# Beta written to the outputs ahead of time and added onto by transfers; two sums of x's parts moved from VectorE to ScalarE and adding transfers

## The chip, the cores and the metric

The kernel runs on one core of a Trainium2 chip, in float32. A time is the device time of one execution in microseconds (us). A figure given as a median is over several executions. The trace is of one further execution taken with the hardware profiler, and it has a time of its own. Engines are named as the profile names them: PE (TensorE), DVE (VectorE), ACT (ScalarE), POOL (GpSimd) and SP (SyncE). PEld is PE's loading of weights. A `q` after an engine's name (SPq, POOLq) means its instruction queue, for instructions such as a transfer's issue.

## The reference

Two layers of cross attention over a batch of eight. `x` is (8, 100, 1024): eight batches of 100 query rows. `ctx` is (8, 1444, 512): 1444 context rows per batch.

```python
# layer 0
Q = x @ Wq + bq;  K = ctx @ Wk + bk;  V = ctx @ Wv + bv
w = softmax(Q K^T / 32, over the context rows)
x = x + (w V) @ Wo + bo
# layer 1, with weights of its own
q, k, v = x @ Wq + bq, ctx @ Wk + bk, ctx @ Wv + bv
w = softmax(q k^T / 32, over the 100 query rows)
y = w v + x
out = (y - mean(y)) * rsqrt(var(y) + 1e-6) * gamma + beta      # over the 1024 features
```

`gamma` and `beta` are vectors of 1024 values, the same for every row.

## The kernel before

**Folded weights.** No K or V of 1444 rows is made. The kernel first multiplies weight matrices with each other: `qk0` = Wq Wk^T of layer 0, `vo0` = Wv Wo of layer 0, `qk1` = Wq Wk^T of layer 1 (`weight_products`, in this order; `qk1`'s multiplications come after layer 0's queries). The features of x then meet the 512 features of the context directly: `queries` computes g = W^T x + u for all 800 query rows, `scores` multiplies g with the context, `weighted_rows` multiplies the softmax weights with the context rows, and `project0` or `project1` carries the result back to 1024 features.

**x lies transposed.** `xT` holds x as 128 partitions by 8 chunks of features by 800 rows, so a block of it has features on the partitions. `project0` adds onto `xT` in place, and layer 1's `untransposed` brings each batch back to rows, as a tile `z` of 100 rows by 1024.

**Products with seven multiplications.** Most products are computed as two-by-two blocks with seven block products in place of eight (Strassen's scheme in Winograd's form), which costs sums of blocks beforehand. For `queries` the left blocks A are parts of the folded weights and the right blocks B are four parts of `xT`: B11 and B21 are the first 400 rows (two halves of the features), B12 and B22 the second 400 rows. The sums on the right are T1 = B12 - B11, T2 = B22 - T1, T3 = B22 - B12, and T4 = B21 - T2, which is written over T1. Each has 128 partitions by 1600 elements, 800 KB. T1 and T2 lie in two tiles of the tag `AT`, which the product `vo0` uses just before for sums of its own (`vo_s` in the trace). Layer 0's order in `queries` on PE is: product X from A11 and B11 (16 matmuls named `g_x`), a nested seven-product form of A12 times B21 (`g_z_...`), product Y from S1 and T1 (`g_y`), a further accumulation onto X from S2 and T2 (`g_x`), then the rest. The nested form makes small sums of its own on DVE (in the tile `g_t`, as T1 and T2 also show up in the trace, since both names begin with `g_t`; the shape tells them apart: 128x1600 against 128x400 and 128x256).

**Adding transfers.** The kernel has a helper, `transfer_added(to, t)` (line 572), that issues from POOL a DMA transfer which adds `t` onto `to` in SBUF. It sums scaled rows of weights with it: ACT scales (`scaled_sum`, line 578), the transfers add.

**What sets the order of the work.** PE runs its instructions in the order in which the program writes them (`manual_schedule`). For the other engines and for the transfer queues, a planner orders instructions by its own estimates of when each is ready. It may deviate from the written order: `wv1`'s load, written after those of gamma, beta and `bv1`, is issued ahead of them in the trace. `keep_in_program_order`, and `vector.in_order = True` for DVE, hold instructions so marked in their written order among themselves. Every engine runs its own instructions one after the other, so an instruction that waits holds up all that stands behind it on that engine.

**The end of layer 1.** For each batch, `untransposed` transposes `xT` on PE and DVE makes `z`. For batches 0 to 6 `normalise` (line 1201) then works on `z`: DVE takes mean and variance (`bn_stats`, `bn_aggr`), POOL raises the variance to -0.5 (`rstd`, line 1210), DVE subtracts the mean and multiplies with gamma (line 1211). Then, for batches 0 to 5, ACT multiplies with `rstd` (line 1216) and POOL adds beta (line 1217). For batch 6 DVE does both in one instruction (line 1214). The result is written to `out` by a transfer from POOL's queue (batches 0 to 3) or from SP's (batches 4 to 6). `finish` is called so that batches 0 to 2 are finished while batch 4 is worked on, batch 3 during batch 5, and batches 4, 5 and 6 while batch 7's weighted rows are multiplied. Batch 7 has a path of its own, `project_last` (line 1235). PE multiplies in three parts (`ol`: 384, 512 and 129 columns), DVE makes the mean and then `centred` part by part, ACT squares and sums each part (line 1264), POOL raises to -0.5 (`rstd_last`, line 1272), and DVE applies it with beta in two halves, each written by a transfer of its own (from SP and from ACT).

**Loading gamma and beta.** Both come into SBUF, spread over 128 partitions, with transfers from POOL's queue (line 1357), as does `bv1` (line 1359), when layer 1's queries begin. They lie in two tiles named `vectors_0` and `vectors_1`. `wv1`, 2 MB, is loaded in the same place of the program (line 1361).

Of the kernel before, what the change touches and what calls it, by code (L numbers as in the profile page):

```python
# [26 lines left out]
AF = mybir.ActivationFunctionType  # L27
ALU = mybir.AluOpType
# [4 lines left out]
B, T, E = 8, 100, 1024  # L33
# [15 lines left out]
SETS = (range(0, 4), range(4, 7), range(7, 8))  # L49
# [6 lines left out]
def two_layer_cross_attention(ctx: ExitStack, tc: tile.TileContext, a: dict, out: bass.AP):  # L56
    nc = tc.nc
# [16 lines left out]
    def unit(name):  # L74
        return stream.tile([P, E + L], F32, tag="unit", name=name)
# [104 lines left out]
    def combine(to, x, y, op, engine=vector):  # L180
        for t, p, q in zip(to, x, y):
            engine.tensor_tensor(t, p, q, op)
# [389 lines left out]
    def transfer_added(to, t):  # L572
        nc.gpsimd.dma_start(out=to, in_=t, accum_op=ALU.add)
# [85 lines left out]
    def queries(layer, w, u, between=None):  # L659

        H, nb, h = EC // 2, 2, GT // 2
        A11, A12, A21, A22 = ([w[:, k * H : (k + 1) * H, j * 256 : j * 256 + 256]] for j in range(2) for k in range(2))
        B11, B21, B12, B22 = ([xT[:, k * H : (k + 1) * H, g * GT : g * GT + GT]] for g in range(2) for k in range(2))
        S1, S2 = (
            [(unit if layer else row)(f"g{layer}_s{n}")[:, :E].rearrange("p (c l) -> p c l", c=H)] for n in (1, 2)
        )
        dst = [None, None]  # L670

        def put(r, g, banks):
            for j in range(2):
                c = 2 * r + j
                nc.scalar.activation(dst[g][:, c, :], banks[j][:, :GT], AF.Identity, bias=u[:, c : c + 1])  # L675

        def add(r, g, banks):
            for j in range(2):
                to = dst[g][:, 2 * r + j, :]
                vector.tensor_tensor(to, to, banks[j][:, :GT], ALU.add)  # L680

        def parts(R, G):
            def part(r, c, ps):
                return dst[G][:, 2 * R + r, c * h : c * h + h], ps[:, :h]

            def put(r, c, ps):
                c0 = 2 * R + r
                nc.scalar.activation(*part(r, c, ps), AF.Identity, bias=u[:, c0 : c0 + 1])

            def add(r, c, ps):  # L690
                to, got = part(r, c, ps)
                vector.tensor_tensor(to, to, got, ALU.add)

            return put, add

        def pair(n):

            return [(bank2 if layer and n == "y" else bank)(f"g{layer}_{n}{j}") for j in range(2)]

        def product(banks, lhs, rhs, fresh):  # L700
            half_product(banks, lhs, rhs, fresh, nb, GT)

        t = None

        def inner(n, lhs, rhs, put, add, right=None, at=0, left=None):
            spare = bank if layer else bank2
            return inner_product(f"g{layer}_{n}", lhs, rhs, nb, GT, t[:, at:], put, add, right, left, spare=spare)

        def four(t):

            return [[t[:, n, :].rearrange("p (i t) -> p i t", i=2)] for n in range(4)]

        def steps():
            nonlocal t
            S3, S4 = A21, A12
            if layer:
                combine(S1, A21, A22, ALU.add)
                yield
                combine(S2, S1, A11, ALU.subtract)
                yield  # L720
                combine(S3, A11, A21, ALU.subtract)
                yield
            T1, T2 = ([wide(f"g{layer}_t{n}")] for n in (1, 2))
            if layer:
                combine(T1, B12, B11, ALU.subtract)
                yield
            t = unit(f"g{layer}_t")
            T3 = [work.tile([P, LC, GT], F32, tag="gT", name=f"g{layer}_t3", bufs=3)]
            dst[:] = [work.tile([P, LC, GT], F32, tag="gT", name=f"g{layer}T_{g}", bufs=3) for g in range(2)]
            X = pair("x")  # L730
            product(X, A11, B11, True)
            put(0, 0, X)
            yield
            vector.in_order = True
            if layer == 0:

                rooms = t[:, :E].rearrange("p (n c l) -> p n c l", n=4, c=2)
                rooms = [[rooms[:, n]] for n in range(4)]
                _, more = parts(0, 0)
                Z = inner("z", A12, B21, more, more, four(T3[0]), left=rooms)  # L740
                combine(S1, A21, A22, ALU.add)
                combine(T1, B12, B11, ALU.subtract)
                run(Z)
                combine(S2, S1, A11, ALU.subtract)
                combine(T2, B22, T1, ALU.subtract)
                vector.in_order = False
                yield
                vector.in_order = True
                combine(S3, A11, A21, ALU.subtract)
                combine(T3, B22, B12, ALU.subtract)  # L750
            Y = pair("y")
            product(Y, S1, T1, True)
            put(1, 1, Y)
            if layer:

                vector.in_order = False
                yield
                vector.in_order = True
                S4 = A11
                combine(S4, A12, S2, ALU.subtract)  # L760
                _, more = parts(0, 0)
                Z = inner("z", A12, B21, more, more, four(T3[0]))
                combine(T2, B22, T1, ALU.subtract)
                run(Z)
                combine(T3, B22, B12, ALU.subtract)
            else:
                combine(S4, A12, S2, ALU.subtract)
            combine(T1, B21, T2, ALU.subtract)
            vector.in_order = False
            yield  # L770
            product(X, S2, T2, False)
            put(0, 1, X)
            yield
            vector.in_order = True
            V = half_steps(X, S3, T3, False, nb, GT)
            for n, _ in enumerate(inner("w", A22, T1, *parts(1, 0))):
                next(V)
                if layer:
                    yield
                if layer == 0 and n == 1:  # L780
                    between()
                elif layer == 0 and n == 3:

                    add(0, 1, Y)
                    _, more = parts(0, 1)
                    Q = inner("q", S4, B22, more, more, four(T2[0]), E)
            if layer == 0:
                next(Q)
                run(V)
                yield  # L790
                run(islice(Q, 4))
                add(1, 0, X)
                add(1, 1, X)
                run(Q)
                vector.in_order = False
            else:
                run(V)
                add(1, 0, X)
                add(1, 1, X)
                vector.in_order = False  # L800
                yield
                product(Y, S4, B22, False)
                add(0, 1, Y)
            yield

        return dst, steps()


# [392 lines left out]
    def normalise(s):  # L1201
        b, z = s["b"], s["z"]
        stats = small.tile([T, 2, 6], F32, tag="stats", name=f"stats_{b}")
        for j in range(2):
            nc.vector.bn_stats(stats[:, j, :], z[:, j * 512 : (j + 1) * 512])
        mv = small.tile([T, 2], F32, tag="mv", name=f"mv_{b}")
        nc.vector.bn_aggr(mv, stats.rearrange("p a n -> p (a n)"))
        rstd = small.tile([T, 1], F32, tag="rstd", name=f"rstd_{b}")
        nc.vector.tensor_scalar(rstd, mv[:, 1:2], EPS, None, ALU.add)
        nc.gpsimd.tensor_tensor(rstd, rstd, mhalf[:T], ALU.pow)  # L1210
        nc.vector.scalar_tensor_tensor(z, z, mv[:, 0:1], gamma[:T], ALU.subtract, ALU.mult)
        if b == B - 2:

            nc.vector.scalar_tensor_tensor(z, z, rstd, beta[:T], ALU.mult, ALU.add)
        else:
            nc.scalar.activation(z, z, AF.Copy, scale=rstd)  # L1216
            nc.gpsimd.tensor_tensor(z, z, beta[:T], ALU.add)  # L1217

        (nc.gpsimd if b < SETS[1][0] else nc.sync).dma_start(out=out[b], in_=z)

    def finish(s):

# [134 lines left out]
        nc.gpsimd.dma_start(out=t, in_=a[f"L1_xattn_{name}"].partition_broadcast(P))  # L1357
    for j, t in enumerate(bv1):
        nc.gpsimd.dma_start(out=t, in_=a["L1_xattn_bv"][j * 512 : (j + 1) * 512].partition_broadcast(P))
    wv1 = weights.tile([P, LC, E], F32, tag="w", name="wv1")  # L1360
    nc.gpsimd.dma_start(out=wv1, in_=a["L1_xattn_Wv"].rearrange("(c p) e -> p c e", p=P))  # L1361

# [54 lines left out]
```

## Time and profile before

| What | Value |
|---|---|
| Time, median of 3 runs | 633.31 us (632.94 to 633.76) |
| The profiled execution's own time | 633.67 us |
| Its span, first to last instruction | 631.6 us |
| Granted clock of PE | 0.996 of full |
| PE busy | 621.8 us (98%), 4142 matmuls |
| DVE busy | 482.4 us (76%) |
| ACT busy | 175.4 us (28%) |
| POOL busy | 101.5 us (16%) |
| Moved by DMA | 139.84 MB, 221 GB/s over the span |
| Beta added by POOL (line 1217) | 6 instructions, 2.36 us each |

The span is the profiled execution from its first to its last instruction, and the execution's own time is 2.1 us more. "Busy" counts only instructions at work. A wait is listed with the instruction that waited, on the left of an arrow, and the one that ended its wait, on the right. In a timeline a row gives start and duration in us, then engine, line, operation, output and inputs, shapes and how many instructions the row merges; a bracket gives the idle time before it and what ended it. A helper's line stands for all that go through it: line 96 is every DVE instruction issued through `vector`, line 163 every matmul of a block product. Tiles appear by name with their numbers left out.

### The profile page before, as it was taken

The numbers are of one execution on the slowest core, as the hardware profiler recorded it, in microseconds if no ns is written. First come the engines' busy times: TensorE is split into PE (matmuls) and PEld (weight loads), VectorE is DVE, ScalarE is ACT, GpSimd is POOL, SyncE is SP. The second block draws the span as 40 slices with busy tenths as digits, with TensorE's granted clock in tenths as the row PEclk, the third lists the DMA queues.
The fourth block names the chain that finished last, engine by engine and source line by source line (L and its number), as shares of the span: only waits on it lengthen the run. The fifth ranks groups of instructions, "written<-read, shape, count | busy, mean of one in ns | idle before, by whom it ended". The sixth has DMA issues, their size and how long they took to land.

```text
span 631.6 us, 10604 instructions
## 1 busy us (share of the span) xinstructions
PE 621.8 (98%) x4142; PEld 534.8 (85%) x4142; DVE 482.4 (76%) x993; ACT 175.4 (28%) x403; POOL 101.5 (16%) x135
## 2 busy tenths in 40 slices
PE   9999999999999999999999999999999999999994
PEld 8886467688986999999989666757999999999992
DVE  2977789996875797666758686968777659898886
ACT  1333112324304234423230001113433240328302
POOL 2110101112230000000000001008111220544052
PEclk9999999999999999999999999999999999999998
DMA  9969988336999799888942308266889990697202
GB/s 283 285 146 312 306 233 273 68 80 113 198 326 380 281 315 307 320 302 308 310 160 84 105 0 328 94 195 193 303 303 310 315 311 11 203 338 256 97 22 84
DMA packets 52952, 139.84 MB, mean 221 GB/s; under 512 B 4450, under 2 KB 8802, under 8 KB 52902
## 3 DMA queue, kind: packets, MB, share of 16 engines
q1 hardware_dynamic: 46792, 120.85, 55.7%
q0 software_dynamic: 5712, 17.84, 13.0%
q8 instruction: 33, 0.54, 0.3%
q10 hardware_dynamic: 398, 0.47, 0.2%
q14 instruction: 17, 0.14, 0.1%
HBM read 123.36 MB, written 3.28 MB: 201 GB/s over the span
## 4 chain that ended last, share of the span: by engine, by line
PE 96%; DVE 1%; issue 1%; POOL 1%; ACT 0%; DVEq 0%; POOLq 0%
PE s L929 25%; PE A L900 25%; PE qk_x L163 7%; PE o_x L163 5%; PE g_x L163 4%; PE vo_x L163 3%; PE o_y L163 3%; PE g_y L163 3%; PE qk_y L163 2%; PE qk_z L163 2%; PE o_z L163 1%; PE o_w L163 1%; PE qk_w L163 1%; PE vo_y L163 1%; PE vo_z L163 1%
## 5 line engine op out<-in xcount | busy, mean ns | idle before, releaser
L900 PE MATMUL A<-w,c 120*128 120x100 f32 (+1 forms) x1536 | 249.7, 265 | 0.0
L900 PEld LDWEIGHTS A<-w,c 120*128 120x128 f32 (+1 forms) x1536 | 218.0, 190 | 2.8
L96 DVE STREAM_TRANSPOSE w<-prob 32x384 f32<-32x384 f32 (+1 forms) x256 | 143.7, 561 | 27.9 <-ACT prob L968 9.7
L929 PE MATMUL s<-cT,g1T 128*100 128x131 f32 (+2 forms) x592 | 122.8, 296 | 0.0
L929 PE MATMUL s<-cT,g0T 128*100 128x131 f32 (+2 forms) x592 | 122.7, 296 | 0.0
L929 PEld LDWEIGHTS s<-cT,g1T 128*100 128x100 f32 x592 | 78.4, 167 | 8.6 <-issue 0.3
L929 PEld LDWEIGHTS s<-cT,g0T 128*100 128x100 f32 x592 | 78.2, 167 | 8.4 <-PE c L599 0.4
L941 ACT ACTIVATE prob<-s,c 100x393 f32<-100x393 f32 (+2 forms) x64 | 34.5, 560 | 110.5 <-PE s L929 97.3
L1117 ACT ACTIVATE w<-w,negmax 120x100 f32<-120x100 f32 (+1 forms) x96 | 34.8, 364 | 83.0 <-DVE negmax L96 83.0
L961 DVE TENSOR_REDUCE maxima<-prob 100x1 f32<-100x394 f32 (+3 forms) x32 | 16.5, 528 | 24.3 <-ACT prob L941 24.0
L1361 POOL DMA_DIRECT2D wv<-in_L_xattn_Wv x1 | 0.8, 772 | 192.5 <-PE o_x L163 192.5
L163 PE MATMUL qk_x<-qk 128*128 128x256 f32 x128 | 30.2, 384 | 0.0
L1136 POOL TENSOR_TENSOR part<-w 120x500 f32<-120x500 f32 x8 | 10.9, 1366 | 112.8 <-PE s L929 42.3
L163 PEld LDWEIGHTS qk_x<-qk 128*128 128x128 f32 x128 | 23.7, 194 | 3.1 <-ACT qk L437 0.2
L675 ACT ACTIVATE g1T<-g_x,k 128x400 f32<-128x400 f32 x4 | 2.4, 594 | 68.5 <-PE g_x L163 68.4
L1117 ACT ACTIVATION_READ_ACCUMULATOR w<-w,negmax 120x1 f32 (+1 forms) x96 | 17.9, 187 | 0.0
L96 DVE TENSOR_TENSOR xT<-xT,o_x 128x400 f32<-128x400 f32 (+1 forms) x32 | 15.8, 538 | 2.2 <-PE o_x L163 2.0
L1194 PE MATMUL z<-ident,xT 128*100 128x128 f32 x64 | 16.3, 273 | 0.0
L1217 POOL TENSOR_TENSOR z<-z,vectors 100x1024 f32<-100x1024 f32 x6 | 14.1, 2358 | 8.1 <-ACT z L1216 8.1
L1198 DVE SCALAR_TENSOR_TENSOR z<-vectors,r,z 100x512 f32<-100x512 f32 x16 | 11.8, 740 | 4.8 <-PE z L1194 4.8
L163 PE MATMUL vo_x<-vo 128*128 128x512 f32 x32 | 15.3, 595 | 0.0
L965 ACT ACTIVATE prob<-prob,negmax 100x1444 f32<-100x1444 f32 x8 | 12.0, 1499 | 11.2 <-DVE negmax L963 11.2
(431 smaller groups left out, 995.7 us busy)
## 6 DMA issues: line engine op xcount, KB each, us to landing
cT<-in_ctxT SPq DMA_DIRECT2D x64, 722.0 KB, 6.9
c<-in_ctx SPq DMA_DIRECT2D x48, 768.0 KB, 9.0
c<-in_ctx SPq DMA_DIRECT2D x16, 512.0 KB, 6.4
vo<-in_L_xattn_Wo SPq DMA_DIRECT2D x8, 512.0 KB, 9.6
qk<-in_L_xattn_WqT SPq DMA_DIRECT2D x8, 512.0 KB
qk<-in_L_xattn_WqT SPq DMA_DIRECT2D x15, 256.0 KB, 5.9
c<-in_ctx SPq DMA_DIRECT2D x16, 224.0 KB, 5.5
xT<-in_xT SPq DMA_DIRECT2D x2, 1600.0 KB
```

Source lines behind the costliest of these rows:

```text
L96: ins = getattr(nc.vector, op)(*args, **kw)
L163: nc.tensor.matmul(banks[n // per][:, n % per * width : (n % per + 1) * width], lhs[i][:, n * P : (n + 1) * P], rhs[i], start=(fresh and i ...
L900: nc.tensor.matmul(ps[:, k * T : (k + 1) * T], c[m // CQ][:r, m % CQ, k * P : (k + 1) * P], w[:r, m, :], start=(m == 0 and k == 0), stop=( ...
L929: nc.tensor.matmul(banks[n // per][:T, cuts[n] - o : cuts[n + 1] - o], q[:, k, t0 : t0 + T], cT[k][:, cuts[n] : cuts[n + 1]], start=(k == ...
L941: nc.scalar.activation(p[:, part], ps[:T, : part.stop - part.start], AF.Identity, bias=key_bias[layer][:T, b : b + 1], scale=SCALE,)
L961: nc.vector.tensor_reduce(maxima[:, n : n + 1], p[:, part], AX.X, ALU.max)
L965: nc.scalar.activation(p, p, AF.Exp, bias=negmax, accum_out=total)
L1117: nc.scalar.activation(w[:r, m0 + m, :], w[:r, m0 + m, :], AF.Exp, bias=negmax[:r, m : m + 1], accum_out=total[:r, m : m + 1])
L1136: add(part, w[:MR, 0:5, :], w[:MR, 5:10, :], ALU.add)
L1194: nc.tensor.transpose(ps[:T, e * P : (e + 1) * P], xT[:, 4 * j + e, b * T : (b + 1) * T], ident)
L1198: nc.vector.scalar_tensor_tensor(z[:, half], bv1[j][:T], s["r"], ps[:T, :], ALU.mult, ALU.add)
L1217: nc.gpsimd.tensor_tensor(z, z, beta[:T], ALU.add)
```

## The change

Two things are changed.

1. **Beta.** Right after the loads of gamma, beta and `bv1`, seven transfers from POOL's queue write the beta tile, 100 rows of 1024 equal rows, into `out` for batches 0 to 6. In `normalise` the addition of beta is gone for all seven: ACT multiplies with `rstd` (also for batch 6), and a transfer from POOL's queue adds `z` onto what stands in `out`. No output is written from SP's queue in `normalise` any more. Batch 7 stays as it was.
2. **Sums in layer 0's queries.** T1 = B12 - B11 and T2 = B22 - T1 are no longer made by DVE. ACT writes -B11 into T1, an adding transfer adds B12; ACT writes -T1 into T2, an adding transfer adds B22. The two ACT instructions are marked to keep their order, and they are written ahead of the first product of the queries. Layer 1's queries are unchanged.

```diff
@@ queries(): steps, after T1 and T2 are taken
+            if layer == 0:
+                tc.keep_in_program_order(nc.scalar.activation(T1[0], B11[0], AF.Copy, scale=-1.0))
+                transfer_added(T1[0], B12[0])
+                tc.keep_in_program_order(nc.scalar.activation(T2[0], T1[0], AF.Copy, scale=-1.0))
+                transfer_added(T2[0], B22[0])
@@ queries(): layer 0, the nested product
                 combine(S1, A21, A22, ALU.add)
-                combine(T1, B12, B11, ALU.subtract)
                 run(Z)
                 combine(S2, S1, A11, ALU.subtract)
-                combine(T2, B22, T1, ALU.subtract)
@@ normalise()
-        if b == B - 2:
-            nc.vector.scalar_tensor_tensor(z, z, rstd, beta[:T], ALU.mult, ALU.add)
-        else:
-            nc.scalar.activation(z, z, AF.Copy, scale=rstd)
-            nc.gpsimd.tensor_tensor(z, z, beta[:T], ALU.add)
-
-        (nc.gpsimd if b < SETS[1][0] else nc.sync).dma_start(out=out[b], in_=z)
+        nc.scalar.activation(z, z, AF.Copy, scale=rstd)
+
+        nc.gpsimd.dma_start(out=out[b], in_=z, accum_op=ALU.add)
@@ after the loads of gamma, beta and bv1
+    for b in range(B - 1):
+        nc.gpsimd.dma_start(out=out[b], in_=beta[:T])
```

## The prediction

> **What bounds the kernel now.** I read first the chain that ended last, then PE's waits, then timelines around the two places that the change touches. The chain, by engine:
>
> ```profile
> PE 96%; DVE 1%; issue 1%; POOL 1%; ACT 0%; DVEq 0%; POOLq 0%
> ```
>
> All of PE's listed waits (total, times, longest):
>
> ```profile
> PE warm L108 <- DVE ones L105: 1.1, 1, 1.1
> PE g_z_x L163 <- DVE g_t L96: 0.4, 1, 0.4
> ```
>
> PE is the bound until its last matmul ends at 623.3. Time can be won only from the 0.4 us wait and from the tail of 8.3 us behind that matmul, and lost wherever PE is made to wait.
>
> The wait lies in layer 0's queries; the 128x1600 row is T1, which the change takes off DVE:
>
> ```profile
> 104.72 1.81 DVE L96 TENSOR_TENSOR g_t<-xT 128x1600 f32<-128x1600 f32 x1
> ...
> 106.45 0.35 DVE L96 TENSOR_TENSOR g0T<-g0T,g_z_x 128x200 f32<-128x200 f32 x1
> 106.72 0.56 DVE L96 TENSOR_TENSOR g_t<-xT,g_t 128x400 f32<-128x400 f32 x1
> 107.21 0.42 DVE L96 TENSOR_TENSOR g_t<-g_t,qk 128x256 f32<-128x256 f32 x1
> ...
> 107.68 0.94 PE L163 MATMUL g_z_x<-g_t,g_t 128*128 128x200 f32 x4 [0.42 <-DVE g_t L96]
> ```
>
> The tail; the L1217 row is batch 5's beta, the L1211 row batch 6, `mean` and `centred` batch 7:
>
> ```profile
> 617.17 2.35 POOL L1217 TENSOR_TENSOR z<-z,vectors 100x1024 f32<-100x1024 f32 x1 [1.86 <-ACT z L1216]
> ...
> 617.46 3.15 DVE L1211 SCALAR_TENSOR_TENSOR z<-z,mv,vectors 100x1024 f32<-100x1024 f32 x1
> ...
> 618.81 4.48 PE L1259 MATMUL ol<-wv,A1T 128*100 128x512 f32 x16
> ...
> 619.49 1.53 POOL L1210 TENSOR_TENSOR rstd<-rstd,mhalf 100x1 f32<-100x1 f32 x1
> ...
> 620.53 0.20 DVE L96 SCALAR_TENSOR_TENSOR mean<-ol,last 100x1 f32<-100x1 f32 x1
> ...
> 621.05 1.28 DVE L1214 SCALAR_TENSOR_TENSOR z<-z,rstd,vectors 100x1024 f32<-100x1024 f32 x1 [0.31 <-POOL rstd L1210]
> ...
> 623.56 1.00 DVE L96 SCALAR_TENSOR_TENSOR centred<-ol,mean,z 100x512 f32<-100x512 f32 x2
> ```
>
> Two transfers in the list of issues, an adding one and beta's load (last number: us to landing):
>
> ```profile
> vo_L_xattn_bv<-prob POOLq DMA_DIRECT2D x1, 512.0 KB, 6.9
> ```
>
> ```profile
> vectors<-in_L_xattn_beta POOLq DMA_DIRECT2D x1, 512.0 KB, 12.8
> ```
>
> **What the Trainium skill says.** "SBUF — State Buffer", section "Who interferes with whom": a DVE instruction with two SBUF inputs contends with a POOL instruction that reads SBUF, and the loser blocks fully. The trace agrees: L1211 (z and gamma) takes 3.15 us beside the L1217 addition, 1.27 us at its shortest. "DMA: Bandwidth & Descriptors", section "SWDGE vs HWDGE vs iDMA": accumulating transfers go only from GpSimd, so all seven outputs join POOL's queue. The same page's "Rules for kernel authors" wants an accumulating transfer to wait for the earlier one on the same bytes; beta's writes precede the additions by over 140 us, so that wait should be spent; no run here shows it yet.
>
> **The sums T1 and T2.** Off DVE: two instructions of 1.81 us. Onto ACT: two copies of 1600 elements; the 128x1532 copy at line 1230 took 1.455 us, so 1.52 each. Onto POOL: two issues of 0.86 (line 573). Two adding transfers of 800 KB: unloaded, 256 KB landed in 3.3 us and 512 KB in 4.5, which gives 5.9 for 800 KB. The 84.53 one, shown above, took 6.9 beside the loads of `qk1`'s weights, 1.5 times unloaded, and the slowest issued singly 9.5: 9.0 and 12.4 for 800 KB.
>
> Start: the two `AT` tiles come free at 86.2 (DVE's last reading of `vo_s`, 84.78 + 1.42). I let ACT finish its copies first, at 88.83. Then 90.4 first copy, 99.4 landed, 100.9 second copy, 109.9 landed (issue included in landing). PE needs T1 at 110.57, where it is ready 11 us ahead, and T2 at 115.95, 6 us ahead. At 12.4 us each T2 comes at 116.7, 0.7 us after PE's old start. `xT` gives its side in runs of 1600 bytes, the measured ones in runs of 2 or 4 KB; I leave that to the span from 9.0 to 12.4. While the second copy waits, nothing of ACT stands behind it before 104.60. Unloaded the landings are 96.3 and 103.7. Cover is thus some 5.4 us once PE comes 0.6 earlier; past it each us costs one.
>
> The loads of `qk1`'s weights share the engines of these transfers. 1.64 MB at the 284 GB/s of 88 to 92 us is 5.8 us. ACT's first scaling of them is at 105.77; behind the five scalings that end at 108.9 comes g_y's put at 115.48, so 6.5 us are covered. PE needs them at 136.5.
>
> Gain: without T1, DVE's addition starts when `g_z_x` ends (105.91) instead of 106.45, and S2 is ready by 107.15, before PE is through with `g_z_y` (107.26). The 0.42 goes. The next two groups took 0.94 and 0.92 against 0.84 elsewhere; that 0.18 should go too. I take 0.6, bounds 0.4 and 0.6. The later 1.81 (T2) lies beside 5.4 us of PE work: nothing. PE is unstalled until the tail, so the 0.6 is carried there.
>
> **Beta's writes.** Seven issues (0.61 each for `out` before) take 4.3 us on POOL and wait for beta's landing, 379.37 + 12.8 = 392.2. POOL's next work is at 426.97. Even `wv1`'s load, if queued behind them at 396.5, lands 11.6 later, at 408.1. The 2.87 MB at the span's mean 221 GB/s move in 13 us, to 405. DMA moved nothing from 395 to 399; the single context load in the stretch, at 401.50, is used at 426.71. Cost nothing, cover 13 us or more.
>
> **Finishing, batches 0 to 3.** POOL loses its additions (2.36 each) and issues cost 0.86 instead of 0.61; PE waits for none of it. Nothing; no wait of PE for z's buffers shows.
>
> **The tail.** L1217 and L1214 go. L1211 of batch 6 starts at 617.46, takes 1.27, ends 618.7. `mean` needs the first part of `ol`, ended 618.97: 619.0 instead of 620.53, its scaling at 619.3 instead of 622.25. The first `centred` (0.62) and its product (0.56) are over at 620.6. The second waits only for the 512-wide part of `ol`; PE starts loading for the 129-wide part at 622.25, so I put its end at 622.4 and `centred` at 622.5 instead of 623.56. All that follows (squares, POOL's -0.5 power, the two halves, their transfers) hangs on it: 1.05 us won. Bounds 0 and 1.3.
>
> New beside it: batch 6's POOL power waits behind batch 5's issue (617.1 + 0.86) and may run to 619.5; ACT's 1.15 to 620.7; POOL's issue to 621.5, while the last power isn't due before 624.9. ACT's next work, the first square, moves to 620.7, before the second at 623.3. The adding transfer into `out` is not in the trace. From below 5.9, the fastest plain one from POOL's queue; from above 9.8, the slowest, plus 4.1 for a further pass over 400 KB (an adding one of that size): 13.9. I take 7.5, near the plain median 7.1, as HBM must also be read: landed 628.2, or 627.6 with the 0.6. The end itself moves to 631.6 - 1.65 = 629.95. Cover 2.3 us.
>
> **Sum.** 633.67 (the profiled execution, its span and the 2.1 around it) - 0.6 - 1.05 = 632.0. It lay 0.36 above the median, so 631.7 against the runs' 633.31.
>
> **Rivals.** A: one gain fails, because the planner puts other DVE work in the gap or the last additions eat the tail. For it: both gains are a few DVE instructions wide. Against: DVE has 1.9 us of slack before the second `centred`. 633.31 - 0.6 or - 1.05: 632.3 to 632.7, at the worst 633.3.
> B, slower: the second adding transfer makes PE wait at `g_x`. It needs queue order more than bandwidth: if POOL issues it behind the two issues at 107.38 and 108.61, that is after 109.5, it lands 9.0 later at 118.5, 2.55 past 115.95; the 0.6 is swallowed, the tail's 1.05 stays: 634.8. It decides for slower from a landing at 118.3. For it: the order is the planner's estimate. Against: its input is ready 7 us before 107.38.
> C: batch 6's adding transfer sets the end. Above 9.9 us to landing each us costs one; at 13.9, 635.7.
>
> **Chances.** Forecast 0.52, A 0.29, B 0.12, C 0.07. A difference below 0.2% (1.27 us) is about what cannot be told from no change: faster is below 632.04, slower above 634.58. The forecast's own range is 631.0 to 632.1; A adds up to 633.3, and the low edges of B and C 634.2: 0.8 in all. Faster 0.52, same 0.31, slower 0.17.
>
> **What would show it.** PE's list of waits without `g_z_x`, and `g_x` at 115.3 unwaited; L1211 of batch 6 at about 1.3 us; the second `centred` within 0.2 us of `ol`'s second part; beta's writes over before 410. Wrong if PE waits for a DMA in the queries, or if the last packets belong to POOL's queue.

## The result and the profile after

The changed kernel takes 632.43 us (median of 20 runs, 631.93 to 633.29). The kernel before, run beside it, takes 633.34 (632.94 to 634.27, 20 runs). The ratio is 0.9982, with a 95% interval of 0.9976 to 0.9989: 1.1 us won by the ratio and 0.9 by the medians. This is just below the 0.2% that the prediction took as the limit of what a measurement can tell, though the interval leaves out 1. The forecast was 631.7. The direction is right and the gain is too large by half a microsecond: 632.43 lies outside the forecast's own range (631.0 to 632.1), in the part up to 633.3 that the prediction gave to rival A.

The head of the page of the changed kernel, and its chain that ended last. DVE lost 8 us of work, and the chain is PE's even more than before:

```profile
span 630.5 us, 10617 instructions
...
PE 621.6 (99%) x4142; PEld 534.7 (85%) x4142; DVE 474.2 (75%) x990; ACT 179.5 (28%) x406; POOL 97.7 (16%) x141
...
PE 97%; issue 1%; ACT 0%; POOL 0%; DVE 0%; DVEq 0%; POOLq 0%; ACTq 0%
```

PE's waits after the change (total, times, longest). The list is as long as before, and the second line isn't the old one: its releaser is another DVE instruction, and it stands in layer 1's queries.

```profile
PE warm L108 <- DVE ones L105: 1.1, 1, 1.1
PE g_z_x L163 <- DVE qk L96: 0.3, 1, 0.3
```

Layer 0's queries after the change, a timeline (start, us; the bracket is the idle time before and what ended it):

```profile
88.54 1.54 ACT L729 ACTIVATE g_t<-xT 128x1600 f32<-128x1600 f32 x1
...
90.38 1.29 POOL L573 DMA_DIRECT2D g_t<-xT  x1 [5.01 <-ACT g_t L729]
...
103.28 1.54 ACT L731 ACTIVATE g_t<-g_t 128x1600 f32<-128x1600 f32 x1 [13.20 <-DMA g_t<-xT]
...
105.11 1.28 POOL L573 DMA_DIRECT2D g_t<-xT  x1 [13.44 <-ACT g_t L731]
105.84 0.36 DVE L96 TENSOR_TENSOR g0T<-g0T,g_z_x 128x200 f32<-128x200 f32 x1 [1.22 <-ACT g0T L675]
...
107.08 0.94 PE L163 MATMUL g_z_x<-g_t,g_t 128*128 128x200 f32 x4
107.86 0.92 PE L163 MATMUL g_z_w<-g_t,qk 128*128 128x200 f32 x4
```

```profile
115.34 5.54 PE L163 MATMUL g_x<-g_t,g_s 128*128 128x400 f32 x16
```

`g_z_x` at 107.08 has no bracket any more: the 0.42 us wait is gone. The next two groups still take 0.94 and 0.92. The first adding transfer, issued at 90.38, lets ACT start at 103.28. In the list of issues the two have a median of 11.1 us to landing; one by one they take 12.8 and 9.4. So T2 lands at 105.11 + 9.4 = 114.5, and PE needs it at 115.34. The room is 0.8 us.

The new wait, in a timeline of layer 1's queries, first before and then after the change:

```profile
390.79 0.84 PE L163 MATMUL g_z_x<-xT,qk 128*128 128x200 f32 x4
...
391.74 0.36 DVE L96 TENSOR_TENSOR g1T<-g1T,g_z_x 128x200 f32<-128x200 f32 x1 [1.52 <-PE g_z_x L163]
```

```profile
390.18 0.84 PE L163 MATMUL g_z_x<-xT,qk 128*128 128x200 f32 x4
...
391.48 0.36 DVE L96 TENSOR_TENSOR g1T<-g1T,g_z_x 128x200 f32<-128x200 f32 x1 [1.87 <-PE g_z_x L163]
...
392.00 3.22 POOL L1360 DMA_DIRECT2D out<-vectors  x6 [11.66 <-DMA vectors<-in_L_xattn_beta]
392.25 0.42 DVE L96 TENSOR_TENSOR qk<-g_t,qk 128x256 f32<-128x256 f32 x1
392.72 0.94 PE L163 MATMUL g_z_x<-g_t,qk 128*128 128x200 f32 x4 [0.34 <-DVE qk L96]
```

DVE's addition starts 0.95 us after the start of PE's group before, and 1.30 us after it in the changed kernel; its idle time grew from 1.52 to 1.87. It does the same work on the same input. What stands behind it, `qk`, is late by as much, and PE waits 0.34. Beta's writes start on POOL at 392.00, after DVE was already late. Nothing in this kernel's diff touches layer 1's queries.

The tail after the change:

```profile
617.14 0.88 POOL L1218 DMA_DIRECT2D out<-z  x1 [2.06 <-ACT z L1216]
...
617.21 1.27 DVE L1215 SCALAR_TENSOR_TENSOR z<-z,mv,vectors 100x1024 f32<-100x1024 f32 x1
...
618.56 4.48 PE L1258 MATMUL ol<-wv,A1T 128*100 128x512 f32 x16
...
618.83 0.22 DVE L96 SCALAR_TENSOR_TENSOR mean<-ol,last 100x1 f32<-100x1 f32 x1 [0.34 <-PE ol L1258]
...
620.39 0.87 POOL L1218 DMA_DIRECT2D out<-z  x1 [1.48 <-ACT z L1216]
...
622.20 1.23 DVE L96 SCALAR_TENSOR_TENSOR centred<-ol,mean,z 100x512 f32<-100x512 f32 x2 [1.72 <-PE ol L1258]
...
626.66 0.57 ACTq L1274 DMA_DIRECT2D out<-z  x1
```

L1215 is the old L1211, batch 6's product. It takes 1.27 instead of 3.15. The mean is made at once behind the first part of `ol`, and the second `centred` begins 3.64 us after the start of `ol`'s second row (4.75 before), behind an idle time of 1.72. Batch 6's adding transfer is issued at 620.39 and takes 5.0 to landing, so it is over by 625.4, ahead of the last issue at 626.66. In the list of issues (KB each, median us to landing):

```profile
out<-vectors POOLq DMA_DIRECT2D x7, 400.0 KB, 7.9
out<-z POOLq DMA_DIRECT2D x7, 400.0 KB, 6.7
g_t<-xT POOLq DMA_DIRECT2D x2, 800.0 KB, 11.1
```

**Where the time went.** The start of layer 0's first `g_x` differs by up to 1.6 us from one profiled execution to another (98.9 to 100.5), more than what is looked for. So I cut each trace into stretches from there on, between starts of PE groups and the start of the last issue (ACT's row of `out<-z`). In the kernels of this study that share a part, they repeat within 0.03 us. Only the last row of the table varies (3.6 to 4.1), and with no part of the change:

| us | before | after |
|---|---|---|
| first `g_x` of layer 0 to `g_z_x` of layer 1 | 291.19 | 290.76 |
| from there to the second row of `ol` | 228.02 | 228.38 |
| from there to the last issue | 9.19 | 8.10 |
| from there to the end of the span | 3.59 | 3.88 |

The first queries win 0.43, layer 1's queries lose 0.36 of it, and the tail wins 1.09: 1.16 in all.

### The profile page after: what moved, and what is told of

Same layout as the page of the kernel before. It is cut to its first block, busy times and chain, and to the rows that moved or that the text cites. A ratio compares the mean times of both kernels' runs of the same rounds, so it can differ in the third digit from the quotient of the medians.

```text
span 630.5 us, 10617 instructions
## 1 busy us (share of the span) xinstructions
PE 621.6 (99%) x4142; PEld 534.7 (85%) x4142; DVE 474.2 (75%) x990; ACT 179.5 (28%) x406; POOL 97.7 (16%) x141
## 4 chain that ended last, share of the span: by engine, by line
PE 97%; issue 1%; ACT 0%; POOL 0%; DVE 0%; DVEq 0%; POOLq 0%; ACTq 0%
PE s L933 25%; PE A L904 25%; PE qk_x L163 7%; PE g_x L163 5%; PE o_x L163 5%; PE vo_x L163 3%; PE o_y L163 3%; PE g_y L163 3%; PE qk_y L163 2%; PE qk_z L163 2%; PE o_z L163 1%; PE o_w L163 1%; PE qk_w L163 1%; PE vo_y L163 1%; PE vo_z L163 1%; PE z L1198 1%
## 5 line engine op out<-in xcount | busy, mean ns | idle before, releaser
L96 DVE TENSOR_TENSOR w<-w,rtotal 120x400 f32<-120x400 f32 (+1 forms) x24 | 14.1, 586 | 0.7
```

What stands on the lines that cost most here:

```text
L96: ins = getattr(nc.vector, op)(*args, **kw)
```

## The experiments

**1. The full change again, and each part alone.** The full change, run beside the parts on one chip:

> The changed kernel itself, beside its parts. Its profile had lost 0.43 us at the first queries and 1.1 us in the tail, and got back 0.35 us in layer 1's queries and 0.24 us behind the last issue. Expected: 1.1 us under the kernel before (ratio 0.998); a wait of PE at g_z_x of some 0.3 us near 392 us again if it belongs to this program, none if it was chance in that one execution.

Only the sums (the `queries` part of the diff; beta as before):

```diff
+                tc.keep_in_program_order(nc.scalar.activation(T1[0], B11[0], AF.Copy, scale=-1.0))
+                transfer_added(T1[0], B12[0])
+                tc.keep_in_program_order(nc.scalar.activation(T2[0], T1[0], AF.Copy, scale=-1.0))
+                transfer_added(T2[0], B22[0])
...
-                combine(T1, B12, B11, ALU.subtract)
-                combine(T2, B22, T1, ALU.subtract)
```

> Only the sums T1 and T2 by ACT and adding transfers; beta as before. Theory S (the lateness of DVE in layer 1's queries comes with the moved sums, through the shifted instruction stream or time): the wait near 392 us is there, the gain is 0.43 - 0.35 = 0.1 us. Theory P (it comes with POOL's seven issues of beta's writes): no such wait, the gain is 0.4 us. Both: no wait at g_z_x near 107 us, the tail as before.

Only beta (its writes, and `normalise` as in the change; the sums on DVE as before):

```diff
+    for b in range(B - 1):
+        nc.gpsimd.dma_start(out=out[b], in_=beta[:T])
...
+        nc.scalar.activation(z, z, AF.Copy, scale=rstd)
+        nc.gpsimd.dma_start(out=out[b], in_=z, accum_op=ALU.add)
```

> Only beta's part; the sums as before. Theory S: 1.1 us less than before, no new wait near 392 us. Theory P: 0.35 us of it is lost there, 0.75 us less. Both: the wait of 0.4 us near 107 us as before; L1211 of batch 6 (by its new line number) at 1.3 us; the second centred within 0.2 us of ol's second part.

T1 alone by ACT and an adding transfer; T2 stays on DVE, beta as before:

```diff
+                tc.keep_in_program_order(nc.scalar.activation(T1[0], B11[0], AF.Copy, scale=-1.0))
+                transfer_added(T1[0], B12[0])
...
-                combine(T1, B12, B11, ALU.subtract)
```

> Only T1 by ACT and one adding transfer; T2 stays on DVE, beta as before. If T1 alone made the wait near 107 us, as the prediction has it, this gains as much as both sums (the first run of this set with T1 and T2 moved), with one transfer of 800 KB fewer: 0.1 us by theory S, 0.4 us by theory P. If T2's place on DVE matters to PE too, it gains less, and a wait of PE for DVE shows between 110 and 120 us.

Measured, with the kernel before at 633.84 us (median of 50 runs), and the stretches of the table above:

| kernel | us | ratio, 95% interval | to layer 1's `g_z_x` | to `ol` | to last issue |
|---|---|---|---|---|---|
| full change | 632.89 | 0.9983 (0.9977 to 0.9990) | 290.77 | 228.38 | 8.10 |
| only the sums | 633.78 | 1.0001 (0.9993 to 1.0010) | 290.78 | 228.38 | 9.19 |
| only beta | 632.88 | 0.9984 (0.9977 to 0.9992) | 291.20 | 228.02 | 8.11 |
| T1 alone | 633.35 | 0.9997 (0.9989 to 1.0005) | 290.78 | 228.03 | 9.20 |

Of the three parts only beta's can be told from no change by its times. The sums win 0.42 and lose 0.36, by the stretches. T1 alone wins the whole 0.42; moving T2 wins nothing more. The loss is there without beta's writes and is absent with them alone, which ends the suspicion that POOL's seven issues disturb layer 1's queries. With T1 alone moved it is absent too; T2 alone was not tried. PE's waits of the kernel with only the sums show the same new line:

```profile
PE warm L108 <- DVE ones L105: 1.1, 1, 1.1
PE g_z_x L163 <- DVE qk L96: 0.3, 1, 0.3
```

**2. Why DVE is late 280 us behind the sums.** Around the late addition both traces show the same instructions in the same order. What differs is that DVE has run two instructions fewer before it. So I gave it two back that do nothing, writes of a constant into 128x1 (memsets), first at the places of the two sums:

```diff
                 combine(S1, A21, A22, ALU.add)
+                vector.memset(small.tile([P, 1], F32, tag="pad", name="pad1"), 0.0)
                 run(Z)
                 combine(S2, S1, A11, ALU.subtract)
+                vector.memset(small.tile([P, 1], F32, tag="pad", name="pad2"), 0.0)
```

> The changed kernel, with two tiny DVE instructions (memsets of 128x1) put where the two sums left DVE's order, so that DVE's order has as many instructions again as before; the sums themselves stay on ACT and the adding transfers. In layer 1's queries the changed kernel loses 0.36 us, where DVE's addition into g1T begins 1.87 us after PE's g_z_x instead of 1.52. Theory of the stream (the lateness belongs to where that addition falls in DVE's own sequence of instructions, two places earlier): the wait g_z_x <- DVE qk near 392 goes, the stretch from layer 1's g_z_x to the second row of ol takes 228.02 us again instead of 228.38, and the kernel is 0.36 faster than the changed one, 1.5 below before, ratio 0.9977. Rival (something else that T2's move brings, its transfer or its copy on ACT): the wait stays at 0.3, the stretch at 228.38, the ratio at 0.9983 as for the changed kernel.

632.21 us against 633.88, ratio 0.9977 (0.9969 to 0.9985). This interval overlaps that of the full change (0.9977 to 0.9990), so it is the trace that decides: the stretch is 228.03 and the lateness is gone, as the timeline of layer 1's queries shows:

```profile
390.16 0.84 PE L163 MATMUL g_z_x<-xT,qk 128*128 128x200 f32 x4
...
391.11 0.36 DVE L96 TENSOR_TENSOR g1T<-g1T,g_z_x 128x200 f32<-128x200 f32 x1 [1.52 <-PE g_z_x L163]
...
392.35 0.94 PE L163 MATMUL g_z_x<-g_t,qk 128*128 128x200 f32 x4
```

They might have helped by the timing of layer 0's queries. So they went to the start of the program, 380 us ahead of the late spot:

```diff
     nc.vector.memset(mhalf, -0.5)
+    for n in range(2):
+        nc.vector.memset(const.tile([P, 1], F32, tag=f"pad{n}", name=f"pad{n}"), 0.0)
```

> The changed kernel with the two tiny DVE memsets (128x1) at the start of the program, where DVE makes its constants, some 380 us ahead of the spot that is late and far from either layer's queries. Theory of the stream (only the count of DVE's instructions ahead of the addition matters): as with the two memsets in layer 0's queries, no wait g_z_x <- DVE qk, the stretch from layer 1's g_z_x to the second row of ol 228.02 us, ratio 0.9977. Rival (the two memsets helped because they stood in layer 0's queries, by the order or the timing there): the wait of 0.3 is back, the stretch is 228.38, ratio 0.9983.

632.45 against 634.04, ratio 0.9978 (0.9968 to 0.9988), stretch 228.05, and in PE's list of waits only `warm` is left:

```profile
PE warm L108 <- DVE ones L105: 1.1, 1, 1.1
```

So it doesn't matter at which of the two places the memsets stand, and T2's transfer and its copy on ACT, which were still there, don't make the delay. What these runs leave is how many instructions DVE has ahead of the addition. The trace has a second late spot that fits. Counting DVE's records from 0, semaphore waits included, the late addition is number 703 in the changed kernel, 705 before and with the memsets, and 706 with T1 alone, which has one sum fewer and two semaphore waits more. Number 959, 256 later, is the small operation of line 1213 for one of the batches. It too follows a semaphore wait, and it too starts late, in a timeline of the changed kernel:

```profile
554.62 0.21 DVE L1211 BATCH_NORM_AGGREGATE mv<-stats 100x2 f32<-100x12 f32 x1
555.29 0.15 DVE L1213 TENSOR_SCALAR rstd<-mv 100x1 f32<-100x1 f32 x1 [0.46 <-DVE mv L1211]
```

and of the kernel with the two memsets in the queries, where this operation is number 961:

```profile
554.25 0.21 DVE L1213 BATCH_NORM_AGGREGATE mv<-stats 100x2 f32<-100x12 f32 x1
554.57 0.15 DVE L1215 TENSOR_SCALAR rstd<-mv 100x1 f32<-100x1 f32 x1
```

From the start of the aggregate to it, 0.67 against 0.32: the same 0.35, hidden there because PE doesn't wait for it. In the kernels without the lateness numbers 703 and 959 fall on instructions that come straight behind others on DVE, and they start on time. So a small delay is tied to places 256 records apart in DVE's stream, and it shows where the instruction there follows a wait.

The fetching of instructions would fit, and the trace has a sign for it. It lists packets of 8 KB in a queue that it calls `instruction`; the changed kernel has one between 392 and 400 us (packets, MB, share of the engines):

```profile
q14 instruction: 1, 0.01, 0.2%
```

In each of the four late executions such a packet starts 2.3 to 2.4 us after the late addition and 2.4 to 4.1 us after the late small operation. In the eight others none starts within 27 us after either of the two instructions. The packets thus move together with the delay. That a fetch causes it is not shown.

**3. T1 alone with the whole of beta.** The two parts that win something, without T2's move, which wins nothing:

```diff
+                tc.keep_in_program_order(nc.scalar.activation(T1[0], B11[0], AF.Copy, scale=-1.0))
+                transfer_added(T1[0], B12[0])
...
-                combine(T1, B12, B11, ALU.subtract)
...
+        nc.scalar.activation(z, z, AF.Copy, scale=rstd)
+        nc.gpsimd.dma_start(out=out[b], in_=z, accum_op=ALU.add)
...
+    for b in range(B - 1):
+        nc.gpsimd.dma_start(out=out[b], in_=beta[:T])
```

> T1 on ACT with its adding transfer, T2 left on DVE, and the whole of beta's part. The parts add up if they are independent: 0.42 from the first queries and 1.09 from the tail, nothing lost in layer 1's queries, so 1.5 us below before, ratio 0.9976, half a microsecond faster than the full change. Stretches: layer 0's first g_x to layer 1's g_z_x 290.77, from there to the second row of ol 228.02, from there to the last issue 8.10. If beta's writes bring a wait of their own into layer 1's queries once T1 has left DVE, the middle stretch shows 228.4 and the gain stays at 1.1.

632.16 us against 633.88, ratio 0.9975 (0.9967 to 0.9982). The stretches are 290.78, 228.02 and 8.10: the parts add up, 1.5 us in the stretches. It is the best kernel of the study that has no idle instruction in it, and its ratio is beyond the 0.2%, though its interval isn't. By its time alone it can't be told from the full change (0.9977 to 0.9990) nor from the full change with the memsets; the stretches show the 0.36.

**4. Which part of beta's change wins the tail.** Beta's path changed for batch 5 alone, so that POOL's addition beside batch 6's product is gone, and batch 6's own addition stays on DVE:

```diff
+        if b in (5,):
+            nc.scalar.activation(z, z, AF.Copy, scale=rstd)
+            nc.gpsimd.dma_start(out=out[b], in_=z, accum_op=ALU.add)
+            return
...
+    for b in (5,):
+        nc.gpsimd.dma_start(out=out[b], in_=beta[:T])
```

> The kernel before, with beta's path changed for batch 5 alone: beta written to its output beforehand, ACT's scaling, and the adding transfer; POOL's addition L1217 for batch 5 is gone, batch 6 keeps its addition on DVE, batches 0 to 4 and the sums are as before. Theory (the tail's 1.09 comes from DVE no longer being blocked by POOL's addition): batch 6's addition on DVE takes 1.27 instead of 3.15 and ends at 618.7, the mean of batch 7 is done at about 619, and the second centred comes right behind ol's second row, so the full 1.09, ratio 0.9983. Rival (it comes from taking batch 6's addition off DVE, as such): less than half of it here.

And the other way round: batch 6's addition has left DVE, and POOL's addition of batch 5 stays.

```diff
+        if b in (6,):
+            nc.scalar.activation(z, z, AF.Copy, scale=rstd)
+            nc.gpsimd.dma_start(out=out[b], in_=z, accum_op=ALU.add)
+            return
...
+    for b in (6,):
+        nc.gpsimd.dma_start(out=out[b], in_=beta[:T])
```

> The kernel before, with beta's path changed for batch 6 alone: its addition on DVE (L1214, 1.28) is gone, replaced by ACT's scaling and an adding transfer; POOL's addition for batch 5 stays beside batch 6's product on DVE, which should still take 3.15. Expected: that product ends at 620.6, mean, its scaling and the first centred with its product are over by about 622.2, the second centred begins within 0.3 of ol's second row, so 0.8 to 1.09 us, ratio 0.9983 to 0.9987. Rival (the blocked product is what costs the time): it leaves centred late by half a microsecond or more, and half of the gain or less.

633.09 and 632.89 us against 633.88; ratios 0.9986 (0.9979 to 0.9992) and 0.9986 (0.9980 to 0.9993). The last stretch is 8.08 and 8.11: each half alone wins all of the 1.09, and doing both wins nothing more. Both rivals, which expected half of the gain or less, are refuted. The timeline of the tail with batch 5 alone:

```profile
617.34 1.27 DVE L1211 SCALAR_TENSOR_TENSOR z<-z,mv,vectors 100x1024 f32<-100x1024 f32 x1
...
619.09 1.28 DVE L1218 SCALAR_TENSOR_TENSOR z<-z,rstd,vectors 100x1024 f32<-100x1024 f32 x1
...
622.33 1.23 DVE L96 SCALAR_TENSOR_TENSOR centred<-ol,mean,z 100x512 f32<-100x512 f32 x2 [0.64 <-PE ol L1263]
```

and with batch 6 alone:

```profile
617.71 3.16 DVE L1211 SCALAR_TENSOR_TENSOR z<-z,mv,vectors 100x1024 f32<-100x1024 f32 x1
...
622.70 1.23 DVE L96 SCALAR_TENSOR_TENSOR centred<-ol,mean,z 100x512 f32<-100x512 f32 x2 [0.26 <-PE ol L1263]
```

In the second the product still takes 3.16 beside POOL's addition, and yet `centred` waits for PE's result, and not the result for DVE. The idle time ahead of `centred` is what DVE has to spare: 0.26, 0.64 and, with both, 1.72. The gain ends where it turns positive. This also shows that the 3.15 belongs to POOL's addition beside it: with that gone for batch 5 alone, the same product takes 1.27.

**5. How much room T2's transfer has.** The second adding transfer issued twice, so that B22 is added twice:

```diff
                 transfer_added(T2[0], B22[0])
+                transfer_added(T2[0], B22[0])
```

> The changed kernel with the adding transfer of B22 into T2 issued twice, so that B22 is added twice and T2 isn't the sum that the queries want. It measures how much room the second adding transfer has before PE's g_x. In the changed kernel T2 lands at about 114.5 and g_x begins at 115.34, 0.8 us of room. If the second issue has to wait for the first one's landing, T2 comes 7 to 9.4 us later, 121.5 to 124, and PE waits 6 to 8.5 us at g_x, about that much slower in all; if the two overlap in the queue, 3 to 5 us. If my forecast's 6 us of room held, PE would wait 1 to 3 us.

One execution took 642.65 us, 10.2 more than the changed kernel. PE's waits:

```profile
PE g_x L163 <- DMA g_t<-xT: 7.0, 1, 7.0
PE warm L108 <- DVE ones L105: 1.1, 1, 1.1
PE A L905 <- ACT w L1122: 0.7, 1, 0.7
PE g_z_x L163 <- DVE qk L96: 0.3, 1, 0.3
PE g_z_x L163 <- DVE g_t L96: 0.2, 1, 0.2
```

The extra transfer was issued only when the one before it had landed (8.64 is POOL's idle time), and PE waited 7.0, within the 6 to 8.5 that a room of 0.8 gives:

```profile
115.19 1.28 POOL L573 DMA_DIRECT2D g_t<-xT  x1 [8.64 <-DMA g_t<-xT]
...
122.19 7.95 PE L163 MATMUL g_x<-g_t,g_s 128*128 128x400 f32 x16 [7.02 <-DMA g_t<-xT]
```

The surprise is in the second row: the 16 matmuls take 7.95 instead of 5.54. The table by stretches (busy us and instructions of PE, PEld, DVE, ACT, POOL, then the granted clock, DMA share, GB/s) shows why:

```profile
115.00:122.00 7.00, 0.17 (x1) 0.00 (x0) 0.61 (x1) 2.44 (x5) 3.07 (x3) 0.86 0.80 133
122.00:126.00 4.00, 3.81 (x6) 2.19 (x7) 3.47 (x5) 0.00 (x0) 0.70 (x2) 0.50 0.62 106
126.00:130.00 4.00, 4.00 (x12) 2.07 (x11) 0.00 (x0) 0.50 (x1) 1.04 (x2) 0.89 0.76 131
```

In the trace the granted clock falls while PE stands still, at 120.1, 4.9 us after its last matmul, and it is 0.50 until 126.9, so for the first 4.7 us of work. Half the clock for 4.7 us loses 2.35 (an estimate from these two figures), and the 16 matmuls took 2.4 longer. The stall of 7.0 cost 7.0 + 2.4. By the stretches, the way to layer 1's `g_z_x` is 9.8 longer than in the changed kernel, which is these 9.4 and the new wait of 0.2, and the stretch behind it is 1.0 longer, with the new wait of 0.7 in it. (The first `g_x` started 0.5 earlier here.)

The 0.2 shows a second tight spot. It lies near 107 us, before the extra transfer was issued:

```profile
103.44 1.54 ACT L731 ACTIVATE g_t<-g_t 128x1600 f32<-128x1600 f32 x1 [13.87 <-DMA g_t<-xT]
...
105.50 0.36 DVE L96 TENSOR_TENSOR g0T<-g0T,g_z_x 128x200 f32<-128x200 f32 x1 [1.39 <-ACT g0T L675]
...
106.74 0.94 PE L163 MATMUL g_z_x<-g_t,g_t 128*128 128x200 f32 x4 [0.17 <-DVE g_t L96]
```

T1's transfer let ACT's second copy start 4.53 us after the start of the first `g_x`, against 3.86 in the changed kernel. ACT's own `g0T` stood behind the copy, DVE's addition waited 1.39 for it instead of 1.22, and PE waited 0.17. So the changed kernel has about 0.5 us of room there (an estimate: 0.67 later cost 0.17), less than the 0.8 in front of T2.

## Why the prediction was right, and where it wasn't

**PE is the bound; beta's writes and the finishing of batches 0 to 3 cost nothing.** Right. Beta's seven issues take 3.74 us from 392.00 and land 7.9 us after issue (median); the last has landed at 405.5. The middle stretch with beta alone is 228.02, as without. The first adding transfer is issued at 549.59, so the wait for the earlier write, which the Trainium skill's page "DMA: Bandwidth & Descriptors" asks for (section "Rules for kernel authors"), costs nothing here, as the prediction expected.

**The tail, 1.05.** Right: 1.09 measured. L1211 takes its 1.27, and the second `centred` begins 3.64 us after the start of `ol`'s second row, where 622.5 stood for 3.69. The reason given, "L1217 and L1214 go", is true but more than is needed: either alone is enough. The Trainium skill's page "SBUF — State Buffer" (section "Who interferes with whom") has it that a DVE instruction with two SBUF inputs contends with a POOL instruction that reads SBUF. Four kernels agree: the product takes 3.15 and 3.16 with POOL's addition beside it, and 1.27 twice without.

**Batch 6's adding transfer, 7.5 with bounds of 5.9 and 13.9.** Too pessimistic: 5.0, below the lower bound; it stays off the end. Rival C isn't near.

**The gain in the first queries, 0.6.** The wait of 0.42 went, and its 0.42 is what the stretch shows. The other 0.18 did not come: the two groups still take 0.94 and 0.92 with no wait ahead of them, so they never belonged to the wait. The lower part of the bounds, 0.4, was the right one.

**The transfers of T1 and T2, 9.0 each, T2 ready at 109.9 with a cover of some 5.4.** The chain of steps was right, its size wrong: 12.8 and 9.4, against a worst case of 12.4 each. T2 came 0.8 us ahead of PE, and 0.35 to 1.2 in the five profiled executions that issue its transfer once. That "nothing of ACT stands behind" the second copy "before 104.60" did not hold either: the copy came so late that it ran from 103.28 to 104.82. That all this cost nothing was closer than the forecast said; the 7.0 us stall of the last experiment shows what stood behind it, and that "past it each us costs one" is too little: there it cost 1.3.

**"PE is unstalled until the tail, so the 0.6 is carried there."** This is the step that failed. In layer 1's queries 0.36 of the 0.42 was lost again, by an instruction that the change doesn't touch: what changed is its place in DVE's stream, and with two idle instructions ahead of it the loss went. This is what rival A allowed for in size ("one gain fails", 632.3 to 632.7; 632.43 came), but not by its cause: neither did the planner fill the gap, nor the last additions eat the tail.

The difference of 0.73 between forecast and median is thus 0.36 from layer 1, 0.18 from the two groups, less 0.04 from the tail. The other 0.2 isn't settled. The medians differ by 0.9, the ratio gives 1.1 and the stretches 1.16, so it may be no more than scatter of the medians. It is also of the size by which the end of the span behind the last issue differs between profiled executions (3.59 in that of the kernel before, on which the sum was made, and up to 4.06 elsewhere).

## What to carry to other kernels

Where PE is busy 98% of the span, look for a gain in the waits of PE's list and in the idle tail, and no further: DVE lost 8 us of work here and the kernel 1.1. Two edits that relieve the same late instruction don't add up; ask which one is needed, by the idle time that appears in front of the instruction. And when a gain in one stage seems to be lost in another that the change doesn't touch, cut both traces into stretches between the same instructions: differences of a few tenths stand out there that a span hides.

## What was not expected of the hardware

- A DVE instruction behind a wait started 0.35 us late at two places 256 records apart in DVE's stream, in the four executions with this count of DVE's instructions (the changed kernel twice, the sums alone, the doubled transfer), and at neither place in the eight kernels with another count; two idle memsets ahead of it, at either of two places, took it away. An 8 KB packet of the queue `instruction` followed the late ones within 4.1 us, and none followed the others within 27 us. What it is inside DVE stays open.
- In a stall of 7.0 us PE's granted clock fell to 0.50 after 4.9 us and stayed there for the first 4.7 us of work (one execution).
- Adding transfers of 400 KB into HBM, in the seven profiled executions that have them for all batches, against the plain writes of the same batches from the same queue (five executions): batch 0 5.6 to 6.7 us to landing against 6.8 to 7.1, batch 1 8.6 to 10.5 against 8.3 to 9.9, batch 2 8.9 to 10.3 against 6.8 to 7.2, batch 3 8.1 to 8.7 against 4.8 to 6.8. So some were 2 to 3 us slower than a plain one. They are issued some 3 to 5 us earlier than the plain ones, and what part of this belongs to the adding was not tested. At the end (batches 4 to 6) they took 4.9 to 5.4.
- Two adding transfers of 800 KB into SBUF took 12.8 and 9.4 us to landing beside loads, and their issues 1.29 and 1.28 on POOL, where the prediction had 0.86.
